# Expert rows added to their tokens in DRAM by an accumulating scatter, in a perceiver layer with a mixture of experts

## The chip, the core and the metric

The kernel runs on one core of one Trainium2 chip. The time is device microseconds of one execution, first to last instruction plus what lies around them. Times before: 2608.23, 2605.57 and 2600.91 us, median 2605.57 us. The profile is of a separate execution of 2611.01 us.

The core has a matrix engine (PE), a vector engine (DVE), an activation engine (ACT), a general engine (POOL, also called GpSimd) and a queue engine (SP) that only issues transfers. Each takes its instructions in a fixed order, and an instruction that waits holds up all behind it. Transfers (DMA) run on 16 engines of their own, whoever issues them.

## The reference, cut to what matters

One layer of a perceiver with 512 tokens of width 512: cross attention on a context of 8192 rows, a state-space block with its MLP, and a mixture of experts.

```python
x = x + xattn(layernorm(x), ctx, ctx, ...)      # 16 heads of 64, keys and values from ctx
x = x + ssm_and_mlp(layernorm(x), ...)          # scan over 512 tokens, then a gated MLP
x = x + ffn(layernorm(x), ...)

def ffn(x):                                     # 512 tokens, 16 experts, two per token
    top_vals, top_idx = top_k(x @ router_w.T, 2)
    gates = sigmoid(top_vals)
    # moe[n] = sum over the two experts e of token n: gate * (silu(x gate_e) * (x up_e)) @ down_e
    return moe + (silu(x @ sg.T) * (x @ su.T)) @ sd.T       # plus one shared expert
```

Every weight and the data are float32. The kernel splits each operand into a high and a low float16 half and takes three matmuls for a product (high by high, high by low, low by high).

## The kernel before

**First pass of the attention (`filler`).** Heads are taken in pairs, two pairs a pass. In the first pass the 8192 context rows come in 16 chunks of 512. `ctx_first` loads a chunk in float32 (L230), splits it (L232 to L235) and writes the halves to DRAM for later passes (L236). `kproj_units` and `vproj_units` project keys and values (L251 to L253, L275 to L277) and write them to DRAM. `smax_units` takes a first score with the high halves only (L300), copied by ACT (L305), for a running maximum on DVE (L311, L313). After chunk 0 `first_norm` normalises x and `qproj` projects the queries; the scores of chunk 0 are then spread between the projections of chunk 1. The order on PE is written out by hand in this part: a generator yields its parts, and a list `side` holds score work from which `pump` takes a piece every few projections. On the other engines a scheduler orders the instructions. Weights are loaded by `stage_w` and split by `split_w` (L176, L177).

**Main pass.** Scores, exponentials and products with V, unit by unit, with the projections of later passes filled in by a rate. Beside it `weight_prep` zeroes DRAM scratch and splits the later weights. This takes the time from about 240 to 2100 us. The tail, with the state-space block, the MLP, the router and the experts, follows.

**Router and experts.** The expert of a token is found from the logits; a running count gives each (token, choice) a slot in a table of 23 blocks of 128 rows (16 experts and 7 blocks for overflow). `sg` holds these slots, `gt` the gates. Eight indirect transfers on POOL (L1201), one per group of 128 tokens and choice, scatter the split rows (`xf`, 2 KB each) into the DRAM table `xd_d`. They all write one tensor, so each waits for the one before. `moe_in` loads the 128 rows of a block through SP (L1208), transposes them on PE (L1212) and copies them (`xk`). `moe_up` and `moe_down` do the matmuls (L1225, L1250), `moe_turn` the transposes between; the result is scaled on ACT (`myo`, L1256) and written by SP to row block k of `y_d` (L1257). Weights come in pieces of 512 KB through SP (`wef`, L1089) and are split by ACT and DVE (L1094, L1095) into `we` (18 buffers) or `wpm` (5 buffers, which the shared expert's weights use too, L761). The shared expert (`ffn`, L966 to L978) runs while the scatters go.

Eighteen blocks always run; five more stand behind a test of the overflow count.

**The end.** Eight indirect gathers on POOL (L1285) fetch each token's two results from `y_d`; DVE multiplies by the gate and adds to `x_sb` (L1289); SP writes four output blocks (L1292).

Of the kernel before, what the change touches and what calls it, by code (L numbers as in the profile page):

```python
# [9 lines left out]
F32 = mybir.dt.float32  # L10
AF = mybir.ActivationFunctionType
# [5 lines left out]
P = 128  # L17
# [17 lines left out]
LAST = 8000  # L35


@with_exitstack
def perceiver_layer(ctx: ExitStack, tc: tile.TileContext, a: dict, out: bass.AP):
# [23 lines left out]
    y_d = scr.tile([(16 + NOV) * P, DM], F32, name="y_d")  # L63
    xd_d = scr.tile([(16 + NOV) * P, 2 * DM], F16, name="xd_d")
# [98 lines left out]
    nc.sync.dma_start(bq_sb, a["bq"])  # L163
    nc.sync.dma_start(bk_sb, a["bk"])
    nc.sync.dma_start(bv_sb, a["bv"])
    nc.vector.tensor_scalar(bk_sb, bk_sb, WS, None, ALU.mult)

    def stage_w(src, n, tag, stage=("wst", 1), bufs=2):
        st = sb2.tile([P, NC4, n], F32, name=f"wst_{tag}", tag=stage[0], bufs=stage[1])
        nc.sync.dma_start(st, src)  # L170
        return lambda: split_w(st, n, tag, bufs)
# [254 lines left out]
    def filler():  # L426
# [23 lines left out]
        for g in range(NPASS):  # L450
            pr = (2 * g, 2 * g + 1)
            if g == 0:
                wk0 = load_w(a["Wk"][0], P, "k", bufs=4)
                nct = ctx_first(0)
                wk = [wk0, load_w(a["Wk"][1], P, "k", ("p32", 3), bufs=4)]
                wv = load_w(a["Wv"][0], 256, "v", ("p32", 3))
                nc.sync.dma_start(x_sb, a["x"])
                wq = [load_w(a["Wq"][p], P, "q", ("t2k", 4)) for p in pr]
            else:
                wk, wv, wq = nw  # L460
                qh = [qproj(p, w) for p, w in zip(pr, wq)]
                yield 2 * 2592
            runm = [None, None]
            ks = [[None] * NCH for _ in pr]
            for c in range(NCH):
# [6 lines left out]
                if nxt < NPASS * NCH:  # L472
                    nct = ctx_first(nxt) if nxt < NCH else ctx_load(nxt % NCH)
# [9 lines left out]
                if g == 0 and c == 0:  # L483
                    first_norm()
                    qh = [qproj(p, w) for p, w in zip(pr, wq)]
                    yield 2 * 2592
                if c == 2:
                    for p, q in zip(pr, qh):
                        qplace(p, *q)
                side += [smax_units(c, i, qh[i][0], ks[i][c], runm, g == 0) for i in range(2)]  # L490
# [117 lines left out]
    for m in range(NSTEP):  # L608
        n = NLAST * NSTEP + m
        if m % 4 == 0:  # L610
            load(n // 4 + 1)
        cur = scores(u, m, loads[n // 4], sp, True)
        while len(pend) > 1:
            drain()
        pend.append((u, m, cur))
        if m == 0:
            tl = tail(tc, a, out, const, scr, ident, x_sb, mlp_d, oT, y_d, xd_d, (ps_s, ps_o, ps_x, bank_j))
        for _ in range(2):
            if m >= 1 and not ready:
                ready = next(tl)  # L620
# [12 lines left out]
def tail(tc, a, out, const, scr, ident, x_sb, mlp_d, oT, y_d, xd_d, psums):  # L633
# [494 lines left out]
    xf = const.tile([P, 4, 2, DM], F16, name="xf", tag="big16")  # L1128
    nc.scalar.copy(xf[:, :, 0, :], u_sb)
    nc.vector.tensor_tensor(xf[:, :, 1, :], u_sb, xf[:, :, 0, :], ALU.subtract)  # L1130
# [68 lines left out]
    for i in range(4):  # L1199
        for j in range(2):  # L1200
            nc.gpsimd.indirect_dma_start(  # L1201
                out=xd_d[:], out_offset=bass.IndirectOffsetOnAxis(ap=sg[:, j, i : i + 1], axis=0),
                in_=xf[:, i].rearrange("p x d -> p (x d)"), in_offset=None,
            )

    def moe_in(k):
        xd = g2.tile([P, 2, NC4, P], F16, name="xd", bufs=3)
        nc.sync.dma_start(xd, xd_d[k * P : (k + 1) * P, :].rearrange("t (x d m) -> t x d m", x=2, d=NC4))  # L1208
        pt = bank_j([P, 2, NC4, P], F16, "pxd")
        for x in range(2):  # L1210
            for d in range(NC4):
                nc.tensor.transpose(pt[:, x, d, :], xd[:, x, d, :], id16)  # L1212
        xk = g2.tile([P, 2, NC4, P], F16, name="xk", bufs=2)
        nc.scalar.copy(xk, pt)
        return xk
# [30 lines left out]
    def moe_down(k, gT, ws):  # L1246
# [9 lines left out]
        nc.scalar.activation(yo, py, AF.Copy, scale=IW)  # L1256
        nc.sync.dma_start(y_d[k * P : (k + 1) * P, :], yo)  # L1257
# [24 lines left out]
    for i in range(4):  # L1282
        for j in range(2):
            yg = g2.tile([P, DM], F32, name="yg", tag="yo", bufs=4)
            nc.gpsimd.indirect_dma_start(  # L1285
                out=yg, out_offset=None, in_=y_d[:],
                in_offset=bass.IndirectOffsetOnAxis(ap=sg[:, j, i : i + 1], axis=0),
            )
            nc.vector.scalar_tensor_tensor(  # L1289
                x_sb[:, i, :], yg, gt[:, i, j : j + 1], x_sb[:, i, :], ALU.mult, ALU.add  # L1290
            )
        nc.sync.dma_start(out[:, i, :], x_sb[:, i, :])  # L1292
# [69 lines left out]
```

## Time and profile before

| what | value |
|---|---|
| median of three runs | 2605.57 us (2600.91 to 2608.23) |
| the profiled execution | 2611.01 us, its span 2609.3 us |
| busy share of PE, DVE, ACT, POOL | 91%, 79%, 75%, 2% |
| granted PE clock, mean | 0.973 |
| DMA, moved and mean rate | 531.43 MB, 204 GB/s |
| transfers of SP's queue | 352148 packets, 523.69 MB |
| transfers of POOL's queue | 1280 packets, 4.20 MB |

The page of a profile shows the span in 40 slices, the busy groups of instructions, and the chain of work that ended last. A timeline row gives start, length, engine, line, operation, output and input, and in brackets how long the engine stood idle before it and what ended that. A row of the waits gives the waiting instruction, what released it, and the sum, the number and the longest in us. SPq is SP issuing a transfer; POOL's DMA_INDIRECT is the making of a transfer's descriptors, and the transfer itself follows. PE's matmuls overlap: rows of 0.38 us start every 0.216 us.

### The profile page before, as it was taken

Reading aid. Unit: us, or ns where it says so; the run is one execution under the profiler, and the core shown is the slowest. Engines: PE = TensorE matmul, PEld = TensorE weight load, DVE = VectorE, ACT = ScalarE, POOL = GpSimd, SP = SyncE. Lnnn points to the kernel's source line nnn. Section 1 sums busy time; section 2 is a strip of 40 time slices with the busy share of each in tenths; the row PEclk is TensorE's granted clock in tenths of the full one; section 3 lists DMA queues with packets and bytes.
Section 4 is the critical chain, followed back from the end, with each engine's and each line's share of the span. In section 5 each row is a group of like instructions: output and inputs, shape, how many; then the busy total and the mean of one; then the engine's idle time right before and its main releaser. Section 6 shows DMA issues by size and latency. Waiting matters only on the chain. (4 is left out here: it accounts for less than half of the span.)

```text
span 2609.3 us, 54424 instructions
## 1 busy us (share of the span) xinstructions
PE 2383.2 (91%) x21806; PEld 1676.5 (64%) x21806; DVE 2062.4 (79%) x2403; ACT 1949.2 (75%) x3734; POOL 44.3 (2%) x58
## 2 busy tenths in 40 slices
PE   7999899999999999999999998997877688998895
PEld 3555577776677777767777777995665466665442
DVE  6776588888888888878888778997899999533785
ACT  5787788888788888868888888997776476333784
POOL 2000000000000000000000000000000000001001
PEclk9999999999999999999999999999989899999998
DMA  7974677778687778778877655877510222766896
GB/s 270 312 259 138 231 212 231 229 235 241 199 234 235 226 221 251 226 199 228 236 221 213 175 156 148 207 205 192 159 41 25 97 81 82 260 225 217 293 331 208
DMA packets 353688, 531.43 MB, mean 204 GB/s; under 512 B 25107, under 2 KB 218835, under 8 KB 353301
## 3 DMA queue, kind: packets, MB, share of 16 engines
q1 hardware_dynamic: 352148, 523.69, 65.8%
q0 software_dynamic: 1280, 4.20, 0.5%
q8 instruction: 173, 2.83, 0.5%
q14 instruction: 87, 0.70, 0.1%
HBM read 397.68 MB, written 126.94 MB: 201 GB/s over the span
## 5 line engine op out<-in xcount | busy, mean ns | idle before, releaser
L377 DVE TENSOR_TENSOR phl<-p,phl 128x1024 f16<-128x1024 f32 x512 | 626.7, 1225 | 193.2 <-ACT phl L374 181.0
L372 ACT ACTIVATE p<-pss 128x512 f32<-128x512 f32 x1024 | 597.7, 622 | 114.5 <-PE pss L365 42.2
L305 ACT ACTIVATE sf<-psx 128x512 f16<-128x512 f32 x1024 | 558.5, 625 | 70.9 <-PE psx L300 70.1
L364 PE MATMUL pss<-qhh,k 128*128 128x256 f16 x2048 | 481.0, 275 | 14.3 <-ACT phl L374 12.0
L365 PE MATMUL pss<-qlm,kb 128*128 128x256 f16 x2048 | 479.7, 274 | 0.9 <-DMA kb<-k_d 0.9
L313 DVE TENSOR_TENSOR runm<-runm,sf 128x2048 f16<-128x2048 f16 x240 | 292.3, 1219 | 51.7 <-ACT sf L305 51.5
L394 PE MATMUL po<-v,phl 128*128 128x130 f16 x4096 | 322.7, 220 | 3.9 <-DVE oq L407 3.4
L374 ACT ACTIVATE phl<-pss 128x512 f16<-128x512 f32 x512 | 312.8, 611 | 0.0
L394 PEld LDWEIGHTS <-phl 128*128 128x128 f16 x4096 | 271.0, 98 | 61.6 <-issue 14.8
L275 PE MATMUL psv<-wh_v,ctxc 128*128 128x256 f16 x1024 | 282.0, 275 | 7.3 <-ACT wh_v L176 3.2
L276 PE MATMUL psv<-wl_v,ctxc 128*128 128x256 f16 x1024 | 280.8, 274 | 1.2 <-DVE wl_v L177 1.2
L277 PE MATMUL psv<-wh_v,ctxc 128*128 128x256 f16 x1024 | 280.9, 274 | 0.0
L364 PEld LDWEIGHTS <-k 128*128 128x128 f16 x2048 | 200.9, 98 | 66.0 <-issue 20.0
L365 PEld LDWEIGHTS <-kb 128*128 128x128 f16 x2048 | 201.4, 98 | 53.0 <-issue 14.6
L300 PE MATMUL psx<-khl,qh 64*128 64x512 f16 x1024 | 208.9, 386 | 17.6 <-ACT sf L305 12.2
L922 PE MATMUL py<-hs,ident 128*128 128x256 f32 x512 | 144.0, 437 | 73.5 <-DVE hs L919 73.5
L397 PE MATMUL po<-v,phl 128*128 128x65 f16 x4096 | 208.5, 193 | 2.5 <-DVE phl L377 2.5
L251 PE MATMUL psk<-ctxc,wh_k 128*128 128x512 f16 x512 | 198.0, 387 | 9.9 <-ACT ctxc L234 8.1
L376 DVE CAST phl<-p 128x1024 f16<-128x1024 f32 x256 | 176.0, 687 | 32.2 <-ACT p L372 32.0
L252 PE MATMUL psk<-ctxc,wh_k 128*128 128x512 f16 x512 | 196.3, 383 | 0.8 <-DVE ctxc L235 0.7
L253 PE MATMUL psk<-ctxc,wl_k 128*128 128x512 f16 x512 | 196.3, 383 | 0.0
L922 PEld LDWEIGHTS py<-hs,ident 128*128 128x128 f32 x512 | 107.2, 217 | 107.0 <-DVE hs L919 87.0
(304 smaller groups left out, 3774.6 us busy)
## 6 DMA issues: line engine op xcount, KB each, us to landing
v<-v_d SPq DMA_DIRECT2D x128, 520.0 KB
k<-k_d SPq DMA_DIRECT2D x256, 256.0 KB
ctxc<-ctx_d SPq DMA_DIRECT2D x96, 512.0 KB
wef<-in_gu_dram SPq DMA_DIRECT2D x72, 512.0 KB
v_d<-vs SPq DMA_DIRECT2D x128, 260.0 KB
k_d<-khl SPq DMA_DIRECT2D x128, 256.0 KB
kb<-k_d SPq DMA_DIRECT2D x128, 256.0 KB
wpm<-w_d SPq DMA_DIRECT2D x48, 512.0 KB
```

The lines of the kernel that those rows point to most:

```text
L275: nc.tensor.matmul(ps[:, t, :], lhsT=ct[i // 2][:, 0, i % 2, sl], rhs=wh[:, i, :], start=i == 0, stop=False)
L276: nc.tensor.matmul(ps[:, t, :], lhsT=ct[i // 2][:, 0, i % 2, sl], rhs=wl[:, i, :], start=False, stop=False)
L277: nc.tensor.matmul(ps[:, t, :], lhsT=ct[i // 2][:, 1, i % 2, sl], rhs=wh[:, i, :], start=False, stop=i == NC4 - 1)
L305: nc.scalar.activation(dst, ps, AF.Copy, scale=1.0 / (8.0 * WS))
L313: nc.vector.tensor_tensor(r, r, sf, ALU.max)
L364: nc.tensor.matmul(ps[:, hh], lhsT=k[:, hh, sl], rhs=qhh[:, hh, qs], start=True, stop=False)
L365: nc.tensor.matmul(ps[:, hh], lhsT=b[:, hh, sl], rhs=qlm[:, hh, qs], start=False, stop=True)
L372: nc.scalar.activation(p32[:, i], pss[i], AF.Exp, scale=sc)
L374: nc.scalar.activation(ph[:, i], pss[i], AF.Exp, scale=sc)
L377: nc.vector.tensor_tensor(pl, p32, ph, ALU.subtract)
L394: nc.tensor.matmul(o, lhsT=ph[:, i, hh, qs], rhs=vv, start=first, stop=False, **kw)
L922: nc.tensor.matmul(py[:, j, :], lhsT=ident, rhs=hs[:, n, 1:], start=k == 0, stop=False)
```

## The change

Three parts, of which the first is in no summary of it.

1. **First pass.** The loads of the biases `bq`, `bk`, `bv` move from the head of SP's queue to where they are needed. The second K weights and the V weights are loaded right after chunk 0, into buffers that the main pass uses later, then chunk 1, then x and the Q weights. The first norm and the Q projection move from after chunk 0 to after chunk 1, and the scores of chunk 0 come straight after them, drained before chunk 2.
2. **Scatters.** A row of `xd_d` grows by 8 bytes to `XR` = 1028 halfwords: the token's row number and its gate over 64 (`IW`). Empty slots get, in `weight_prep`, the number of one of 128 spare rows and a zero gate. The eight scatters are declared independent of each other, and go by choice: the gate column of `xf` is written for choice 0, four scatters, then for choice 1, four scatters. Every load of `xd` waits for all eight.
3. **Experts and end.** Rows are loaded, and results stored, through POOL's queue. The store is an indirect transfer that adds the 128 rows, scaled by their gates, to the rows of `sum_d`; `sum_d` is set to `x_sb` before the first. The gathers and adds at the end are gone: `sum_d` is copied to the output from DRAM to DRAM.

In the built program POOL's order among the experts is: the eight scatters, the row loads of experts 0 to 3, then in turn the add of expert k and the row load of expert k+4. That load waits for the add (it reuses its buffer); each add waits for the one before.

```diff
+XR = 2 * DM + 4
-    y_d = scr.tile([(16 + NOV) * P, DM], F32, name="y_d")
-    xd_d = scr.tile([(16 + NOV) * P, 2 * DM], F16, name="xd_d")
+    sum_d = scr.tile([NQ + P, DM], F32, name="sum_d")
+    xd_d = scr.tile([(16 + NOV) * P, XR], U16, name="xd_d")
...
-    nc.sync.dma_start(bq_sb, a["bq"])
-    nc.sync.dma_start(bk_sb, a["bk"])
-    nc.sync.dma_start(bv_sb, a["bv"])
-    nc.vector.tensor_scalar(bk_sb, bk_sb, WS, None, ALU.mult)
...
-                wk = [wk0, load_w(a["Wk"][1], P, "k", ("p32", 3), bufs=4)]
-                wv = load_w(a["Wv"][0], 256, "v", ("p32", 3))
+                wk1, wv = stage_w(a["Wk"][1], P, "k", ("k", 2), bufs=4), stage_w(a["Wv"][0], 256, "v", ("k", 2))
+                nc.sync.dma_start(bk_sb, a["bk"])
+                nc.vector.tensor_scalar(bk_sb, bk_sb, WS, None, ALU.mult)
+                nxt0 = ctx_first(1)
+                wk, wv = [wk0, wk1()], wv()
                 nc.sync.dma_start(x_sb, a["x"])
-                wq = [load_w(a["Wq"][p], P, "q", ("t2k", 4)) for p in pr]
+                wq = [stage_w(a["Wq"][p], P, "q", ("v", 3)) for p in pr]
+                nc.sync.dma_start(bq_sb, a["bq"])
+                nc.sync.dma_start(bv_sb, a["bv"])
...
-                if g == 0 and c == 0:
+                if g == 0 and c == 1:
                     first_norm()
-                    qh = [qproj(p, w) for p, w in zip(pr, wq)]
+                    qh = [qproj(p, w()) for p, w in zip(pr, wq)]
                     yield 2 * 2592
+                    side += [smax_units(0, i, qh[i][0], ks[i][0], runm, True) for i in range(2)]
...
-                side += [smax_units(c, i, qh[i][0], ks[i][c], runm, g == 0) for i in range(2)]
+                if g or c:
+                    side += [smax_units(c, i, qh[i][0], ks[i][c], runm, g == 0) for i in range(2)]
+                if (g, c) == (0, 1):
+                    while len(side) > 2:
+                        yield from pump()
...
+        none = sb2.tile([P, 2, 1], mybir.dt.int32, name="none", bufs=1)
+        nc.gpsimd.memset(none, 0)
+        nc.gpsimd.iota(none[:, 0], pattern=[[0, 1]], base=NQ, channel_multiplier=1)
         for k in range(16 + NOV):
-            nc.sync.dma_start(xd_d[k * P : (k + 1) * P, :], zero)
-            if k >= 16 + MOV:
-                nc.sync.dma_start(y_d[k * P : (k + 1) * P, :], zero.bitcast(F32))
+            rows = slice(k * P, (k + 1) * P)
+            nc.sync.dma_start(xd_d[rows, 0 : 2 * DM], zero.bitcast(U16))
+            nc.sync.dma_start(xd_d[rows, 2 * DM : XR], none.rearrange("p a o -> p (a o)").bitcast(U16))
...
+        nc.sync.dma_start(sum_d[NQ : NQ + P, :], zero.bitcast(F32))
...
+    sent = []
+    for j in range(2):
+        nc.vector.tensor_scalar(xf[:, :, XR - 2 : XR].bitcast(F32), gt[:, :, j : j + 1], IW, None, ALU.mult)
+        for i in range(4):
+            d = nc.gpsimd.indirect_dma_start(
                 out=xd_d[:], out_offset=bass.IndirectOffsetOnAxis(ap=sg[:, j, i : i + 1], axis=0),
-                in_=xf[:, i].rearrange("p x d -> p (x d)"), in_offset=None,
+                in_=xf[:, i], in_offset=None,
             )
+            for o in sent:
+                tc.declare_no_dep(d.ins, o.ins, reason="every slot is one token's: the rows differ")
+            sent.append(d)
...
-        xd = g2.tile([P, 2, NC4, P], F16, name="xd", bufs=3)
-        nc.sync.dma_start(xd, xd_d[k * P : (k + 1) * P, :].rearrange("t (x d m) -> t x d m", x=2, d=NC4))
+        xd = g2.tile([P, XR], U16, name="xd", bufs=4)
+        r = nc.gpsimd.dma_start(xd, xd_d[k * P : (k + 1) * P, :])
...
-        nc.scalar.activation(yo, py, AF.Copy, scale=IW)
-        nc.sync.dma_start(y_d[k * P : (k + 1) * P, :], yo)
+        row, gate_ = slot.pop(k)
+        nc.scalar.activation(yo, py, AF.Copy, scale=gate_)
+        nc.gpsimd.indirect_dma_start(
+            out=sum_d[:], out_offset=bass.IndirectOffsetOnAxis(ap=row, axis=0), in_=yo, in_offset=None,
+            compute_op=ALU.add,
+        )
...
+    nc.sync.dma_start(sum_d[0:NQ].rearrange("(p i) d -> p i d", i=4), x_sb)
     moe(range(16 + MOV), lambda k: expert(k) if k < 16 else overflow(regs[k - 16]))
...
-    for i in range(4):
-        for j in range(2):
-            yg = g2.tile([P, DM], F32, name="yg", tag="yo", bufs=4)
-            nc.gpsimd.indirect_dma_start(
-                out=yg, out_offset=None, in_=y_d[:],
-                in_offset=bass.IndirectOffsetOnAxis(ap=sg[:, j, i : i + 1], axis=0),
-            )
-            nc.vector.scalar_tensor_tensor(
-                x_sb[:, i, :], yg, gt[:, i, j : j + 1], x_sb[:, i, :], ALU.mult, ALU.add
-            )
-        nc.sync.dma_start(out[:, i, :], x_sb[:, i, :])
+    nc.sync.dma_start(out, sum_d[0:NQ].rearrange("(p i) d -> p i d", i=4))
```

More of the change, by code (lines that the diff above doesn't have):

```diff
@@ L10 @@
 F32 = mybir.dt.float32
+U16 = mybir.dt.uint16
 AF = mybir.ActivationFunctionType
@@ L162, in perceiver_layer @@
     bv_sb = L.tile([P, NPAIR], F32, name="bv_sb")
-    nc.sync.dma_start(bq_sb, a["bq"])
-    nc.sync.dma_start(bk_sb, a["bk"])
-    nc.sync.dma_start(bv_sb, a["bv"])
-    nc.vector.tensor_scalar(bk_sb, bk_sb, WS, None, ALU.mult)
     def stage_w(src, n, tag, stage=("wst", 1), bufs=2):
-        st = sb2.tile([P, NC4, n], F32, name=f"wst_{tag}", tag=stage[0], bufs=stage[1])
+        pool = L if stage[0] in ("k", "v") else sb2
+        st = pool.tile([P, NC4, n], F32, name=f"wst_{tag}", tag=stage[0], bufs=stage[1])
         nc.sync.dma_start(st, src)
@@ L471, in filler @@
                 nxt = g * NCH + c + 1
-                if nxt < NPASS * NCH:
+                if nxt == 1:
+                    nct = nxt0
+                elif nxt < NPASS * NCH:
                     nct = ctx_first(nxt) if nxt < NCH else ctx_load(nxt % NCH)
@@ L616, in perceiver_layer @@
         if m == 0:
-            tl = tail(tc, a, out, const, scr, ident, x_sb, mlp_d, oT, y_d, xd_d, (ps_s, ps_o, ps_x, bank_j))
+            tl = tail(tc, a, out, const, scr, ident, x_sb, mlp_d, oT, sum_d, xd_d, (ps_s, ps_o, ps_x, bank_j))
         for _ in range(2):
@@ L630, in perceiver_layer, with tail @@
         pass
-def tail(tc, a, out, const, scr, ident, x_sb, mlp_d, oT, y_d, xd_d, psums):
+def tail(tc, a, out, const, scr, ident, x_sb, mlp_d, oT, sum_d, xd_d, psums):
     nc = tc.nc
@@ L1127, in tail @@
     ln2(1, xT1, lambda: next(rs0, None))
-    xf = const.tile([P, 4, 2, DM], F16, name="xf", tag="big16")
-    nc.scalar.copy(xf[:, :, 0, :], u_sb)
-    nc.vector.tensor_tensor(xf[:, :, 1, :], u_sb, xf[:, :, 0, :], ALU.subtract)
+    xf = const.tile([P, 4, XR], U16, name="xf", tag="big16")
+    xv = xf[:, :, 0 : 2 * DM].bitcast(F16)
+    nc.scalar.copy(xv[:, :, 0:DM], u_sb)
+    nc.vector.tensor_tensor(xv[:, :, DM : 2 * DM], u_sb, xv[:, :, 0:DM], ALU.subtract)
+    nc.gpsimd.iota(xf[:, :, 2 * DM : 2 * DM + 2].bitcast(I32), pattern=[[1, 4], [0, 1]], base=0, channel_multiplier=4)
     mx = G.tile([P, 4, 8], F32, name="mx8")
@@ L1197, in tail @@
     nc.vector.tensor_copy(oii, oid)
-    for i in range(4):
-        for j in range(2):
-            nc.gpsimd.indirect_dma_start(
+    sent = []
[3 more added lines that the diff above has]
+            d = nc.gpsimd.indirect_dma_start(
                 out=xd_d[:], out_offset=bass.IndirectOffsetOnAxis(ap=sg[:, j, i : i + 1], axis=0),
-                in_=xf[:, i].rearrange("p x d -> p (x d)"), in_offset=None,
+                in_=xf[:, i], in_offset=None,
             )
+            for o in sent:
+                tc.declare_no_dep(d.ins, o.ins, reason="every slot is one token's: the rows differ")
+            sent.append(d)
+    slot = {}
     def moe_in(k):
-        xd = g2.tile([P, 2, NC4, P], F16, name="xd", bufs=3)
-        nc.sync.dma_start(xd, xd_d[k * P : (k + 1) * P, :].rearrange("t (x d m) -> t x d m", x=2, d=NC4))
+        xd = g2.tile([P, XR], U16, name="xd", bufs=4)
+        r = nc.gpsimd.dma_start(xd, xd_d[k * P : (k + 1) * P, :])
+        for o in sent:
+            tc.add_manual_dep(
+                r.ins, o.ins.name, mybir.DependencyInfo(mybir.DependencyClass.Sync, mybir.DependencyReason.DATA),
+                reason="rows of every scatter",
+            )
         pt = bank_j([P, 2, NC4, P], F16, "pxd")
@@ L1211, in moe_in @@
             for d in range(NC4):
-                nc.tensor.transpose(pt[:, x, d, :], xd[:, x, d, :], id16)
+                o = x * DM + d * P
+                nc.tensor.transpose(pt[:, x, d, :], xd[:, o : o + P].bitcast(F16), id16)
         xk = g2.tile([P, 2, NC4, P], F16, name="xk", bufs=2)
         nc.scalar.copy(xk, pt)
+        slot[k] = xd[:, 2 * DM : 2 * DM + 2].bitcast(U32), xd[:, 2 * DM + 2 : XR].bitcast(F32)
         return xk
@@ L1255, in moe_down @@
         yo = g2.tile([P, DM], F32, name="myo", tag="yo", bufs=4)
-        nc.scalar.activation(yo, py, AF.Copy, scale=IW)
-        nc.sync.dma_start(y_d[k * P : (k + 1) * P, :], yo)
+        row, gate_ = slot.pop(k)
[3 more added lines that the diff above has]
+            compute_op=ALU.add,
+        )
     def moe(ks, weights):
@@ L1281, in tail @@
         moe(range(16 + MOV, 16 + NOV), lambda k: overflow(regs[k - 16]))
-    for i in range(4):
-        for j in range(2):
-            yg = g2.tile([P, DM], F32, name="yg", tag="yo", bufs=4)
-            nc.gpsimd.indirect_dma_start(
-                out=yg, out_offset=None, in_=y_d[:],
-                in_offset=bass.IndirectOffsetOnAxis(ap=sg[:, j, i : i + 1], axis=0),
-            )
-            nc.vector.scalar_tensor_tensor(
-                x_sb[:, i, :], yg, gt[:, i, j : j + 1], x_sb[:, i, :], ALU.mult, ALU.add
-            )
-        nc.sync.dma_start(out[:, i, :], x_sb[:, i, :])
+    nc.sync.dma_start(out, sum_d[0:NQ].rearrange("(p i) d -> p i d", i=4))
     es.close()
```

## The prediction

> **What bounds the kernel now.** I read the 40 slices first: PE is 9 tenths busy nearly everywhere, so time can be won only where PE waits and nothing else makes up for it. The change touches three such places: the first 50 us, the router with the scatters of the token rows, and the experts with the end. For each I asked the timeline and the waits who is late. 0.3% of 2605.57 us, 7.8 us, is about what a measurement can tell from no change.
>
> *The start.* Idle time of PE by releaser, window 0 to 20 us, then 20 to 40 (waited for: us, times, longest):
>
> ```profile
> PE psk L251 <- ACT ctxc L234: 8.1, 1, 8.1
> PE psv L275 <- ACT wh_v L176: 3.2, 1, 3.2
> PE psv L276 <- DVE wl_v L177: 1.2, 1, 1.2
> ```
>
> PE starts at 8.12 us, and stops again at 17 us for the V weights.
>
> *The scatters.* Timelines of POOL and SP, and PE's waits from 2352 to 2400 us:
>
> ```profile
> 2352.83 1.15 POOL L1201 DMA_INDIRECT xd_d<-xf,sg  x1 [135.70 <-DVE sg L1184]
> 2356.02 0.97 POOL L1201 DMA_INDIRECT xd_d<-xf,sg  x1 [2.04 <-DMA xd_d<-xf,sg]
> 2362.56 0.96 POOL L1201 DMA_INDIRECT xd_d<-xf,sg  x1 [5.57 <-DMA xd_d<-xf,sg]
> ...
> 2384.12 0.95 POOL L1201 DMA_INDIRECT xd_d<-xf,sg  x1 [2.01 <-DMA xd_d<-xf,sg]
> 2387.22 1.31 SPq L1208 DMA_DIRECT2D xd<-xd_d  x3
> 2388.64 0.37 SPq L761 DMA_DIRECT2D wpm<-rsu_d  x1
> PE pu L703 <- DMA wpm<-rsu_d: 8.8, 1, 8.8
> ```
>
> Each scatter waits for the one before, so eight take 34 us. SP stands at the first load of rows (L1208) until 2387.2; the last weights of the shared expert (rsu_d) are queued behind it, and PE waits 8.8 us for them.
>
> *The experts.* Waits of SP and ACT from 2400 to 2586 us, and one window (length; busy us of PE, PEld, DVE, ACT, POOL; PE clock, DMA share, GB/s):
>
> ```profile
> SPq L1257 <- ACT myo L1256: 66.8, 17, 9.2
> ACT we L1094 <- DMA wef<-in_gu_dram: 20.8, 19, 3.0
> 2500.00:2547.00 47.00, 45.53 (x267) 22.07 (x266) 40.74 (x43) 38.80 (x49) 0.00 (x0) 1.00 0.91 333
> ```
>
> Here PE, DVE, ACT and DMA are all within 18% of full. The copies of the result (myo, L1256) start at 2421.19 and 2585.97 us for the first and the eighteenth: 164.8 us for 17 steps, 9.7 each, but 8.7 to 9.0 where nothing waits. In SP's queue, weight loads stand behind the write of each result (66.8 us in all, much of it harmless because the weight buffers are full).
>
> *The end.* Timeline:
>
> ```profile
> 2585.97 0.60 ACT L1256 ACTIVATE myo<-acc 128x512 f32<-128x512 f32 x1 [6.03 <-PE acc L1250]
> 2591.14 0.98 POOL L1285 DMA_INDIRECT yg<-y_d,sg  x1 [206.07 <-SPq L1280]
> ...
> 2600.84 0.95 POOL L1285 DMA_INDIRECT yg<-y_d,sg  x1 [0.30 <-issue]
> 2604.52 1.54 DVE L1289 SCALAR_TENSOR_TENSOR x_sb<-yg,gt,x_sb 128x512 f32<-128x512 f32 x2 [1.44 <-DMA yg<-y_d,sg]
> ```
>
> From the last result to the end of the span: 2609.3 - 2586.6 = 22.7 us, in which PE does nothing.
>
> **Part 1, the start (moved): -3.5 us.** The three bias loads leave the head of SP's queue (issues at 0.81, 1.27 and 1.73 us; the first weight follows at 2.21), so everything starts 1.4 us earlier. The V weights are issued right behind the second K weights instead of behind x and two ctx_d writes; at the rate of the first loads (cf and the second K weights arrived by 10.7 us) they are in at about 11 us, and PE's waits of 3.2 and 1.2 us go. PE then also avoids running V at half clock after the stall (spacing 0.215 instead of 0.108 us for 12 matmuls, 1.3 us). Sum of gains 7.1. Against it: the norm and the Q projection now come after chunk 1, and chunk 0's scores (16 matmuls, 16 copies L305) follow in one block that no projection covers. Before, chunk 1 held those scores and took 13.0 us on PE (37.2 to 50.2). Now it takes 10.4 without them (24 matmuls of 0.216, 48 of 0.109 us), and the block 6.2: the copies need 16 x 0.51 = 8.2 us on ACT (four take 2.05), and four PSUM banks let PE leave some 2 us before their end. Loss 3.6. Net -3.5, between -5 and 0 (DMA is 0.96 busy from 60 to 85 us and could give some back). What follows until 2100 us is bound by PE and shifts along. 23 small writes of row numbers into xd_d and one zeroed block of sum_d replace five zeroed blocks of y_d; they lie in that stretch, where DMA is 0.67 busy (300 to 2100 us): nothing. If SP were late there, 23 x 0.33 us of issue would count, 8 us.
>
> **Part 2, unordered scatters: -4 us.** Without waits POOL issues at the spacing of the gathers (2591.14 to 2600.84, 7 steps: 1.39 us). But the gate of the second choice is written into the same xf, so that write on DVE waits until the first four scatters have landed. Issued from 2352.8 to 2357.0, with 2.7 to 6.3 us to landing (3.8 median, from the scatters' rows), they are done at about 2362. Behind it on DVE is the split of gg (L970, due at 2357.1), and PE's matmuls L711 wait for that: a new stall of 4.8 us (3 to 7). The other four scatters then land by 2372, the row loads on POOL by 2376, before PE wants rows at 2395. The 8.8 us stall goes, as SP has no row loads any more and rsu_d is issued when its buffer frees. -8.8 + 4.8 = -4.0.
>
> **Part 3, experts' rows and results on POOL's queue: -4 us.** One rule speaks against a gain. The row: SP waits 66.8 us for myo with weights queued behind, and ACT waits 20.8 us for weights. The Trainium skill, *DMA: Bandwidth & Descriptors*, "Rules for kernel authors", says that spreading DMAs over SP, ACT and GpSimd for bandwidth does not help, as all run on the same 16 engines. By it the gain is 0, and the extra bytes cost. By the row, the slow steps (2421.19 to 2464.08 us: 42.9 for four) could come to 9.2 each, -6, and the last three (29.1 us, DMA late) lose up to 1.5 more. Issue, not bandwidth, is what is freed: DMA was 0.86 to 0.88 busy in those slow steps. I take the row, but charge the bytes of part 4.
>
> **Part 4, the add in DRAM (not in the trace).** 18 adds of 256 KB read the destination too: 18 x 0.26 = 4.7 MB, at 333 GB/s 14 us of DMA time if DMA bound every step; it has 9 to 14% free over 165 us (15 to 23 us), so I charge half of the 7.6 us of part 3, which leaves 4. The second question is the round trip. In POOL's order each add is followed by the row load four experts on, which waits for that add (it reuses its buffer), and then by the next add. A step therefore lasts at least the add's landing plus 1.3 us. Nearest row: the plain scatter (L1201) of the same 256 KB, 2.7 us quiet, 6.3 us under load. The skill's *Collectives: The Full Stack*, "The bandwidth ceiling: the fold count and why AG ≠ RS ≠ AR", says an add is 2 reads for 1 write and halves the rate. By the row alone 6.3 us; by the rule the moving part doubles (about 1.6 us more, estimated from 256 KB in five packets per engine at the trace's 0.163 us a packet, each taking turns with one of SP's), so 8 us. Bounds 4 and 12. I take 7: a step of 8.3, below PE's 9. Cost 0.
>
> **Part 5, the end: -9.7 us.** Gone: the write's landing, eight gathers, eight adds on DVE, four output writes (22.7 us). New: the last add starts 0.3 us after the result, lands 4.5 us later in a quiet memory (2.7 to 9), SP issues the copy (0.5), and 1 MB goes from DRAM to DRAM. No row has that; 1 MB at the best slice of the trace (383 GB/s) takes 2.7 us, twice that if read and write share the engines, and a write needs about 3 us to land (2606.4 to 2609.3): 5 to 9, I take 7.7 because a DMA of sixteen 64 KB rows is new here. Sum 13.0, gain 9.7 (3 to 14).
>
> **Sum.** -3.5 - 4 - 4 - 9.7 = -21 us on the profiled execution (2611.01 us, span 2609.3), giving 2590. The median of the runs is 5.4 us below that execution: 2605.6 - 21 = **2584 us**.
>
> **Rivals.**
>
> *A, as forecast* (0.58): 2572 to 2596.
>
> *B, the experts give nothing and the scatters' new wait eats the old stall* (0.22). For it: DVE stands in order behind four scatters, and DMA is 0.91 busy where the experts go well. Against it: two of three stalls are queue order, not bytes. Start and end remain, 13 us; less 2 for a slower stage: 2594.
>
> *C, the add's round trip becomes the bound* (0.20, the other side). Place: POOL's queue between add and row load. Each step costs landing + 1.3 us. It decides against the change when 17 steps exceed 164.8 us plus the 12 us won elsewhere (3.5 + 4 + about 4.7 at an end slowed by the same landing): a landing above 9.1 us. At 10 us: 17 x 11.3 = 192, +27 - 12 = +15, so 2620; at 12 us 2650. For it: an add reads first, DMA is full, and no row shows it. Against it: no plain scatter took over 6.3 us. The spare results and rows (four buffers each) only delay it.
>
> **Chances and range.** Faster by over 0.3% (below 2597.8 us): nearly all of A and three quarters of B, 0.73. Within 0.3%: the rest of B and the edge of C, 0.08. Slower: 0.19. Range 2572 to 2613: A's lower end (experts -8, end -13) up to C's first half.
>
> **What would show it.** Start right: V's first matmul near 15.5 us with no wait, chunk 2's K projection near 46.5 instead of 50.2. Scatters: a DVE wait of about 5 us at the second gate write, no PE wait for rsu_d, first expert's transposes 4 us earlier plus the start's shift. Experts: results every 9.2 to 9.5 us. Add: landing under 8 us, POOL idle before row loads but PE never waiting for xd. End: about 13 us from the last result. Wrong if PE waits on xd in every expert (C), or if DMA stays above 0.95 and ACT's wait for weights grows (B).

## The result and the profile after

| | before | after |
|---|---|---|
| median | 2605.84 us (20 runs) | 2610.32 us (20 runs) |
| ratio | 1 | 1.0018, 95% interval 1.0010 to 1.0027 |
| profiled execution, its span | 2611.01, 2609.3 us | 2607.09, 2605.4 us |
| POOL's queue | 1280 packets, 4.20 MB | 4672 packets, 11.56 MB |

The change costs 4.7 us (2.6 to 7.0), where 21 us of gain were forecast. Single executions of one kernel lie some 6 us to either side of the median, and the two profiled ones lie the other way round (3.9 us). So spans are not compared below; each stage is measured from a mark at its head, and the verdicts come from the ratios. 0.001 of the ratio is 2.6 us.

**Start.** V's first matmul comes at 15.92 us without a wait, where 15.5 was forecast. The next trouble lies behind chunk 1, where x is now normalised and transposed. PE's timeline in the kernel before (first transposes, chunk 1), and in the changed one (transposes, scores, chunk 2):

```profile
28.30 0.60 PE L100 MATMUL pt_x<-ident,xn 128*128 128x128 f32 x4
...
37.22 0.38 PE L251 MATMUL psk<-ctxc,wh_k 128*128 128x512 f16 x1
```

```profile
31.66 1.61 PE L102 MATMUL pt_x<-ident,xn 128*128 128x128 f32 x4
...
37.32 1.12 PE L102 MATMUL pt_x<-ident,xn 128*128 128x128 f32 x4 [3.13 <-DVE vs L281]
...
46.53 0.61 PE L299 MATMUL psx<-khl,qh 64*128 64x512 f16 x4
47.86 7.92 PE L299 MATMUL psx<-khl,qh 64*128 64x512 f16 x16 [0.72 <-ACT sf L304]
55.72 0.61 PE L250 MATMUL psk<-ctxc,wh_k 128*128 128x512 f16 x1
```

PE stands 3.13 us because DVE, in order, is still at V's sums and the splits of the next chunk. Transposes and Q projection take 14.9 us (31.66 to 46.53), where they took 8.9 before (28.30 to 37.22). The block of scores then lasts 9.2 us (46.53 to 55.72; forecast 6.2). It holds 20 scores, not 16: when a piece is used up, `pump` goes on to the next, so the loop that drains chunk 0 also takes the first four scores of chunk 1. Chunk 2's K projection starts at 55.7 us: 50.2 before, 46.5 forecast. The windows of 20 to 60 us (length; busy us of PE, PEld, DVE, ACT, POOL; PE clock, DMA share, GB/s), first before, then after:

```profile
20.00:40.00 20.00, 17.34 (x102) 10.56 (x103) 17.56 (x23) 9.00 (x14) 7.19 (x5) 0.91 0.79 283
40.00:60.00 20.00, 18.60 (x111) 8.83 (x110) 11.85 (x15) 15.61 (x31) 0.00 (x0) 1.00 0.77 259
```

```profile
20.00:40.00 20.00, 15.67 (x102) 10.57 (x100) 16.18 (x30) 8.08 (x13) 1.64 (x2) 0.89 0.89 297
40.00:60.00 20.00, 18.93 (x56) 5.85 (x55) 10.55 (x15) 13.84 (x25) 4.25 (x4) 0.68 0.72 228
```

From 40 to 60 us PE is as busy as before but does 56 recorded matmuls in place of 111, at a granted clock of 0.68. A mark further on is ACT's first copy of K in the fifteenth chunk: 227.2 us before, 231.1 after.

**Scatters.** Waits of the changed kernel from 2350 to 2370 us (waited for: us, times, longest), and POOL's timeline:

```profile
DVE xf L1218 <- DMA xd_d<-xf,sg: 8.1, 1, 8.1
...
PE acc L726 <- DVE gg L985: 7.4, 1, 7.4
```

```profile
2354.89 0.96 POOL L1220 DMA_INDIRECT xd_d<-xf,sg  x1 [0.30 <-issue]
2362.93 1.15 POOL L1220 DMA_INDIRECT xd_d<-xf,sg  x1 [7.09 <-DVE xf L1218]
...
2373.27 2.20 POOL L1233 DMA_DIRECT2D xd<-xd_d  x4 [5.40 <-DMA xd_d<-xf,sg]
```

The four scatters go out back to back and the old wait for rsu_d is gone. But the second gate column (L1218) waits for all four, the split of gg stands behind it on DVE, and PE waits 7.4 us, which had been put at 4.8. From SP's first load of the shared expert's gate weights (rsg_d), which heads the stage, to the first expert's transposes it is 86.8 us in place of 88.9: a gain of 2.1 us in this execution.

**Experts.** From the first expert's transposes to the start of the last result: 2395.4 to 2590.5 us, 195.1 in place of 186.4. From first to eighteenth result: 171.4 in place of 164.8. Four waits of the changed kernel from 2395 to 2606 us, and the adds (issue in ns, min/median/max; then the time to landing):

```profile
POOL xd L1233 <- DMA sum_d<-myo,xd: 68.5, 11, 7.4
ACT we L1109 <- DMA wef<-in_gu_dram: 34.1, 34, 3.7
...
PE pxd L1243 <- ACT mg L1262: 12.8, 7, 3.2
...
PE pxd L1243 <- DMA xd<-xd_d: 2.2, 2, 1.5
```

```profile
L1290 POOL DMA_INDIRECT sum_d<-myo,xd x18: 1544/1822/2220, 2420.1 to 2593.0; - x18
...
DMA to landing us min/median/max: 4.7/7.9/9.1
```

The add lands in 7.9 us at the median, near the 7 that was taken, and PE waits only 2.2 us in all for rows (xd). What PE waits for is ACT, and ACT stands 34 times at pieces of weights that have not landed; before it was 20.8 us, 19 times. To see where in the stage the loss lies, the windows of the first three steps and of the rest (same columns), before and after:

```profile
2421.20:2450.20 29.00, 25.94 (x156) 12.98 (x154) 22.07 (x23) 21.31 (x28) 0.00 (x0) 1.00 0.87 298
2450.20:2586.00 135.80, 121.28 (x687) 58.12 (x685) 106.41 (x110) 99.22 (x122) 0.00 (x0) 0.97 0.82 296
```

```profile
2419.20:2454.50 35.30, 30.54 (x171) 14.56 (x170) 23.88 (x25) 22.42 (x29) 7.41 (x6) 0.90 0.90 263
2454.50:2590.60 136.10, 119.16 (x666) 57.65 (x663) 105.65 (x108) 99.96 (x121) 30.95 (x25) 0.96 0.89 294
```

Three steps take 35.3 us in place of 29.0, with the DMA engines busier (0.90), at 263 GB/s (a figure that leaves out what the adds read, as the last section shows), and with a PE clock of 0.90. ACT's wait for pieces in these steps, before and after:

```profile
ACT we L1094 <- DMA wef<-in_gu_dram: 4.8, 3, 2.4
```

```profile
ACT we L1109 <- DMA wef<-in_gu_dram: 8.8, 4, 2.7
```

The fourteen steps that follow take what they took in these two executions. The experts of the kernel before also run, unchanged in their code, in `e_start`, `e_loads` and `e_loads2`, and there the fourteen last 131.0 to 132.4 us. So a single execution tells this stretch only to some 5 us.

**End.** Timeline of the changed kernel:

```profile
2587.48 1.54 POOL L1290 DMA_INDIRECT sum_d<-myo,xd  x1 [6.57 <-ACT myo L1289]
...
2590.52 0.69 ACT L1289 ACTIVATE myo<-acc,xd 128x512 f32<-128x512 f32 x1 [3.31 <-PE acc L1282]
2593.00 1.55 POOL L1290 DMA_INDIRECT sum_d<-myo,xd  x1 [3.97 <-issue]
2599.06 0.61 SPq L1319 DMA_DIRECT2D out_dram<-sum_d  x1
```

14.2 us from the last result to the end of the span (2591.2 to 2605.4), in place of 22.7. The last add starts 1.8 us after the result, because the one before it must land first: where the adds go in turn to two tables (`e_two_xd7`, below), it starts 0.3 us after.

```profile
2578.28 0.69 ACT L1290 ACTIVATE myo<-acc,xd 128x512 f32<-128x512 f32 x1 [3.31 <-PE acc L1283]
...
2579.25 1.55 POOL L1291 DMA_INDIRECT sum_d<-myo,xd  x1 [2.45 <-ACT myo L1290]
```

### The profile page after: what moved, and what is told of

It is laid out like the page before. It is cut to its first block, busy times and chain, and to the rows that moved or that the text cites. A ratio compares the mean times of both kernels' runs of the same rounds, so it can differ in the third digit from the quotient of the medians.

```text
span 2605.4 us, 54442 instructions
## 1 busy us (share of the span) xinstructions
PE 2386.2 (92%) x21806; PEld 1678.3 (64%) x21806; DVE 2055.6 (79%) x2397; ACT 1950.5 (75%) x3734; POOL 77.1 (3%) x89
## 3 DMA queue, kind: packets, MB, share of 16 engines
q0 software_dynamic: 4672, 11.56, 2.0%
## 5 line engine op out<-in xcount | busy, mean ns | idle before, releaser
L393 PEld LDWEIGHTS <-phl 128*128 128x128 f16 x4096 | 271.7, 98 | 61.9 <-issue 14.8
L364 PEld LDWEIGHTS <-kb 128*128 128x128 f16 x2048 | 201.2, 98 | 52.0 <-issue 14.2
L375 DVE CAST phl<-p 128x1024 f16<-128x1024 f32 x256 | 175.9, 687 | 31.8 <-ACT p L371 31.6
L396 PEld LDWEIGHTS <-phl 128*128 128x128 f16 x4096 | 171.2, 97 | 4.3 <-DVE phl L376 3.6
```

What stands on the lines that cost most here:

```text
L364: nc.tensor.matmul(ps[:, hh], lhsT=b[:, hh, sl], rhs=qlm[:, hh, qs], start=False, stop=True)
L393: nc.tensor.matmul(o, lhsT=ph[:, i, hh, qs], rhs=vv, start=first, stop=False, **kw)
L396: nc.tensor.matmul(o, lhsT=pl[:, i, hh, qs], rhs=vv_, start=False, stop=last, **kw)
```

## The experiments

Each ratio is to the kernel before, from five rounds on one chip, with its 95% interval. Not all kernels ran on the same chip, so kernels are compared by their ratios, and a difference of two ratios carries both intervals.

### The start alone, and the change without it

The pieces are those of part 1 of the change, put into the kernel before (`e_start`) or taken out of the changed one (`e_oldstart`):

```diff
-                if g == 0 and c == 0:
+                if g == 0 and c == 1:
                     first_norm()
```

> The kernel before with the change's first part alone (bias loads, V weights early, first norm and Q projection after chunk 1, chunk 0's scores in one block). Theory L (the late norm and Q projection stall PE and lower its clock): chunk 2's K projection near 55.8 us as in the changed kernel, against 50.2, and the whole +4 us, ratio 1.0015. Forecast: 46.5 us and -3.5 us, ratio 0.9987.

> The changed kernel with the first part undone. Theory L: 4 us faster than the changed kernel, so level with the kernel before (ratio 1.000). Forecast: 3.5 us slower than the changed kernel, ratio 1.003.

Measured: 1.0008 (1.0000 to 1.0015) and 1.0010 (1.0002 to 1.0018). Both put the start at about +2 us, and the forecast's -3.5 is excluded by the first. The mark at the fifteenth chunk is steadier than the totals: in the twelve runs with the new start it lies at 230.5 to 233.5 us, mean 232.0, and in the five with the old one at 227.2 to 229.8, mean 228.7. So the start costs 3.2 us there. In the profiled execution the changed kernel had caught up by the fifth chunk (90.1 against 90.2 us), and lost the time again up to the seventh, where DMA was 0.98 busy from 90 to 125 us (0.91 before). Why just there was not tried.

### Only the early weights

`e_loads` moves the loads and leaves norm and Q projection after chunk 0. `e_loads2` also puts x and the Q weights ahead of chunk 1 (in outline; where the weights are split is left out):

```diff
-                nxt0 = ctx_first(1)
                 nc.sync.dma_start(x_sb, a["x"])
                 wq = [stage_w(a["Wq"][p], P, "q", ("v", 3)) for p in pr]
+                nxt0 = ctx_first(1)
```

> The kernel before with the early half of the first part alone: bias loads late, second K weights and V weights right behind chunk 0, chunk 1 before x and the Q weights; the first norm and the Q projection stay after chunk 0. If the late norm alone makes the start lose: PE's waits for the V weights go (4.4 us), chunk 2's K projection near 46 us, the whole 3 to 5 us less than before, ratio 0.998 to 0.999. Rival (the Q weights and x, now behind chunk 1, come late for the norm after chunk 0): PE waits in the Q projection instead, chunk 2 at 50 us or later, ratio 1.000 or more.

> As e_loads, with x and the Q weights issued ahead of chunk 1. If e_loads gained nothing because x came behind chunk 1 (PE stood 5.8 us for the normalised x), that wait goes too: chunk 2's K projection at 45 to 47 us, the whole 3 to 5 us less than before, ratio 0.998 to 0.999. Rival: chunk 1 is late in turn, or DVE is, and the ratio stays at 1.000.

Measured: 1.0003 (0.9995 to 1.0011) and 1.0035 (1.0022 to 1.0049). The first gains nothing and the second, meant to mend it, is the worst start of all, with the mark at 234.0 us. PE waits for DVE's xn 5.8 us in one and 5.7 in the other:

```profile
PE pt_x L100 <- DVE xn L81: 5.7, 1, 5.7
PE psx L297 <- ACT sf L302: 1.7, 1, 1.7
```

(the waits of PE in `e_loads2` from 20 to 60 us). The 4.4 us that PE stood for the V weights in the kernel before had been cover: while it stood, DVE normalised x (statistics from 13.2 us, xn from 19.6). The wait went, and one for DVE took its place. That the order of the loads was the whole cause is thereby refuted.

### The gate column on POOL

```diff
-        nc.vector.tensor_scalar(xf[:, :, XR - 2 : XR].bitcast(F32), ...
+        nc.gpsimd.tensor_scalar(xf[:, :, XR - 2 : XR].bitcast(F32), ...
```

> The changed kernel with the two gate columns written on POOL in place of DVE, so that only POOL, which waits there anyway, stands behind the first four scatters. Theory G (DVE's wait is what eats the gain of the scatters): PE's wait of 7.4 us for gg goes, the first expert's transposes come 5 to 7 us earlier after the first scatter (38 to 40 us in place of 44.5), and the whole is 5 to 7 us less than the changed kernel, ratio to before 0.9995. Rival: the experts' weights come no sooner, and what is won here is waited for among the experts: under 2 us less, ratio 1.001 or more.

Measured: 0.9990 (0.9981 to 0.9998), 7.3 us (4 to 10 by the two intervals) less than the changed kernel. Waits of PE from 2340 to 2405 us in it:

```profile
PE acc L724 <- ACT gg L984: 1.4, 1, 1.4
PE pg L718 <- DMA wpm<-rsg_d: 0.9, 1, 0.9
PE acc L726 <- DVE gg L985: 0.3, 1, 0.3
```

The 7.4 us are gone, and the stage is 79.9 us long in place of 86.8. One instruction of 0.17 us, on the wrong engine, had cost all that the unordered scatters won.

### Unordered scatters alone

`e_scat_rows` is the kernel before with two edits only (and the scatters in order of choice):

```diff
+            for o in sent:
+                tc.declare_no_dep(d.ins, o.ins, reason="every slot is one token's: the rows differ")
-        nc.sync.dma_start(xd, xd_d[k * P : (k + 1) * P, :]...
+        r = nc.gpsimd.dma_start(xd, xd_d[k * P : (k + 1) * P, :]...
```

> The kernel before with unordered scatters and row loads on POOL alone; rows of 2 KB without number and gate, so no gate column is written; results still stored by SP to a table of their own and gathered at the end. Theory G: the 8.8 us wait for rsu_d goes and no wait on DVE takes its place: 6 to 9 us less than before, ratio 0.9965 to 0.998. Rival: the experts take it back because weights arrive no sooner, ratio 0.999 or more.

Measured: 0.9968 (0.9957 to 0.9980), 8.3 us less than before. It is the fastest of the kernels here that leave nothing out, and it beats the kernel before and the changed one. `e_best` adds the start of `e_loads2` to it:

> e_scat_rows with the start of e_loads2: if both gains hold and add up, 11 to 13 us less than before, ratio 0.995 to 0.996; if the start gives nothing, 0.997 as e_scat_rows.

1.0002 (0.9991 to 1.0012): the same start costs the same 9 us in another kernel.

### Plain stores, and bytes in place of the add

`e_plain` drops `compute_op=ALU.add`. `e_read` and `e_read2` add to it 18 loads of 256 KB that nothing reads:

```diff
+        more = g2.tile([P, DM], F32, name="more", bufs=2)
+        r = nc.gpsimd.dma_start(more, a["gu"][:, k % 16, 0:DM])
+        tc.add_manual_dep(r.ins, res.ins.name, ...)        # e_read2 only: after the expert's result
```

> The changed kernel with plain stores in place of adding ones (leaves out the sum: a token's row holds its last result only). Theories B (the add's reads of the old rows fill the DMA engines, which are the bound) and R (each add waits for the one before, 8 us landing and 2 us of issue, and so sets the step of 10 us): the experts' results come every 9.2 us or less in place of 10.1, the end is 2 us shorter, the whole 10 to 17 us less than the changed kernel, ratio to before 0.995 to 0.998. Rival Q (the queues' new order costs it, rows on POOL and weights running ahead on SP): the experts stay at 10 us a step and only the end's 2 us are won, ratio 1.001.

> The changed kernel with plain stores (leaves out the sum, as e_plain) plus a load of 256 KB per expert through POOL's queue into buffers that nothing reads. Theory B (what the add costs is the DMA time of its reads): the 5 us that plain stores gave are lost again, ratio 1.001 to 1.003. Theory R (the add's own round trip): as e_plain, ratio 0.999 to 1.0005.

> As e_read, with each extra load of 256 KB made to wait for the result of its expert: in e_read they had all run before the experts, so that run was e_plain once more. Theory B (what the add costs is the DMA time of its reads): ratio 1.0015 to 1.003, the results 171 us from first to eighteenth. Theory R (the add's own round trip): as e_plain, 0.9995 to 1.0008.

Measured: `e_plain` 0.9998 (0.9988 to 1.0008), 5.2 us (1.8 to 8.6 by the two intervals) less than the changed kernel. In `e_read` the loads ran at 2227 to 2291 us, before the experts, so it is `e_plain` a second time: 1.0005 (0.9995 to 1.0015). `e_read2` holds them in the experts: 1.0022 (1.0011 to 1.0032), 4.4 us (0.5 to 8.3) more than `e_read` for the same loads at another time. First three steps and the rest, `e_plain` and then `e_read2`:

```profile
2424.10:2457.10 33.00, 29.16 (x160) 14.29 (x159) 23.77 (x25) 22.49 (x28) 5.47 (x6) 0.90 0.84 279
2457.10:2589.50 132.40, 117.60 (x678) 57.16 (x675) 106.08 (x108) 99.45 (x121) 22.92 (x25) 0.99 0.84 304
```

```profile
2422.60:2458.60 36.00, 30.68 (x175) 15.17 (x174) 23.90 (x25) 22.46 (x29) 7.14 (x9) 0.95 0.86 288
2458.60:2594.30 135.70, 115.80 (x661) 55.78 (x659) 106.08 (x108) 99.75 (x121) 30.74 (x39) 0.99 0.86 319
```

256 KB more to read per expert, with no add, lengthen both windows, and cost about what the adds cost. PE waits for no row in `e_read2`, so it is not late rows. That speaks for theory B: the price of 18 adds is some 5 us, and their reads alone can account for it. And `e_plain` itself answers the other half: with no add, and SP freed of results and rows, results still take 165.4 us from first to eighteenth (163.7 in `e_read`), against 159.8 to 164.8 in the four kernels with the experts of before. The freed queue alone brings nothing.

The stages of all kernels that share these parts, each from single executions (the scatters from the first load of rsg_d to the first transposes, the experts from there to the start of the last result, the end behind that result):

| kernels | scatters | experts | first three steps | end |
|---|---|---|---|---|
| as before (`before`, `e_start`, `e_loads`, `e_loads2`) | 88.3 to 89.1 us | 181.7 to 186.4 | 28.1 to 29.0 | 22.0 to 22.9 |
| unordered scatters, rows on POOL (`e_scat_rows`, `e_best`) | 79.0 to 79.3 | 187.1 to 189.2 | 31.6 to 32.0 | 22.2 to 22.4 |
| all of parts 2 and 3, plain stores (`e_plain`, `e_read`) | 86.3 to 88.6 | 187.0 to 188.3 | 32.2 to 33.0 | 12.9 to 13.5 |
| the same with adds (`after`, `e_oldstart`) | 86.8 to 89.6 | 193.2 to 195.1 | 35.3 to 36.1 | 14.2 to 14.8 |

So the adds bring about half of what the first three steps lose. The other half is there without any add, once scatters are unordered and rows come through POOL's queue, which is what rival Q of `e_plain` had in mind. Which of the two makes it, and how, was not tried.

### Is it the round trip of the adds?

`e_two` lets experts add in turn into two tables, and copies row number and gate out of the rows. `e_two_xd7` has seven row buffers in place of the copies (in both, the output leaves out the second table), `e_xd7` the seven buffers with one table, and `e_two_sum` two tables that are added at the end, with the old start:

```diff
-            out=sum_d[:], out_offset=bass.IndirectOffsetOnAxis(ap=row, axis=0), in_=yo, in_offset=None,
+            out=sum_d[k % 2][:], out_offset=bass.IndirectOffsetOnAxis(ap=row, axis=0), in_=yo, in_offset=None,
-                    w = g2.tile([P, 2, 1024], F16, name="we", bufs=18)
+                    w = g2.tile([P, 2, 1024], F16, name="we", bufs=16)
-        xd = g2.tile([P, XR], U16, name="xd", bufs=4)
+        xd = g2.tile([P, XR], U16, name="xd", bufs=7)
```

> The gates on POOL, and the round trip broken: the experts add in turn into two tables (the output leaves out the second table), so that an add waits only for the one two before it, and row number and gate are copied out of the rows, so that a row load waits for no add. The bytes are the same. Theory R (round trip): results every 9.2 us or less, 157 us from first to eighteenth, ratio to before 0.994. Theories B and H: 168 to 172 us as with the gates on POOL alone, ratio 0.998 to 1.000.

> As e_two, with seven buffers for the rows in place of the copies on DVE, which in e_two stood waiting for rows 29 us in all; two of the 18 buffers of split pieces pay for it, which by e_stage costs nothing. An add waits only for the one two before it, a row load for an add seven before. Theory R: results 157 to 163 us from first to eighteenth, ratio to before 0.994 to 0.997. Theory B: 168 to 173 us, ratio 0.9985 to 1.0005.

> The changed kernel with the gates on POOL, one table, and seven row buffers in place of four (16 buffers of split pieces in place of 18). A row load now waits for an add seven experts back, but each add still waits for the one before. If the row load's wait in POOL's queue is the link that costs: results 158 to 164 us from first to eighteenth, ratio 0.995 to 0.9975, as e_two_xd7. If the chain from add to add is the link: 168 to 173 us, ratio 0.998 to 1.000, as with the gates on POOL alone.

> e_two_xd7 made whole: the second table starts from zero, and at the end the two are loaded, added on DVE and written out; the first part of the change is undone. From e_two_xd7 (0.9959) the old start takes 2 us off and the longer end adds 2 to 5 us: ratio 0.995 to 0.997, the end 16 to 19 us after the last result. If the gain of e_two_xd7 was not the chain, 0.999.

| | ratio | first three steps | the rest |
|---|---|---|---|
| e_gatepool (base of these) | 0.9990 | 36.3 us | 134.8 us |
| e_two | 1.0048 (1.0035 to 1.0061) | 31.1 | 140.8 |
| e_two_xd7 | 0.9959 (0.9945 to 0.9974) | 28.2 | 133.5 |
| e_xd7 | 0.9987 (0.9976 to 0.9998) | 35.4 | 131.3 |
| e_two_sum | 0.9995 (0.9982 to 1.0007) | 35.2 | 134.1 |

`e_two` missed by far: its copies stand on DVE for rows that have not landed, 29.3 us in all, and PE waits 13.8 us for DVE's mgT, which stands behind them. `e_two_xd7` met what the round trip foretold, 8 us less. But `e_two_sum` breaks the same two links and its experts take 169.3 us from first to last, near the 171.1 of the base (its end lasts 19.6 us, which uses up what the old start wins). `e_xd7` breaks one link and its ratio moves by less than its interval. So the round trip is not what `e_two_xd7` won: in the profiled executions 8.1 of its 9.5 us lie in the first three steps. There its order on ACT differs. In the built programs the scheduler has put one split of weights between the first two experts' activations (mg) in `e_two_xd7`, three in `e_two_sum`. ACT's wait for pieces in these steps of `e_two_xd7`, and their window:

```profile
ACT we L1110 <- DMA wef<-in_gu_dram: 1.6, 4, 0.9
```

```profile
2416.60:2444.80 28.20, 25.43 (x154) 12.72 (x152) 24.44 (x26) 23.48 (x30) 6.80 (x5) 1.00 0.97 313
```

1.6 us, against 8.8 in the changed kernel and 4.8 in the kernel before; three steps in 28.2 us against 35.3 and 29.0. The same adds are there. `e_two` has the order of `e_two_xd7`, and its three steps are short too (31.1). That ACT's order makes the difference between these kernels is read from their traces; an order written by hand was not tried. The order is not what sets the changed kernel apart from the kernel before: that one has three splits in this place as well, and takes 29.0 us. With the same order, the pieces are waited for longer.

### Pacing the weights, and deeper staging

The lead of the loads over the experts (pieces issued when a result starts, less six for each result so far) falls from 25 to 9 in the kernel before, as SP stands at results, and stays at 18 to 25 in the changed one up to its last three steps. `e_pace` forces a falling lead, `e_stage` gives two more staging buffers:

```diff
+                if 31 <= nload[0] < 108:
+                    tc.add_manual_dep(r.ins, results[int((nload[0] - 31) / 5.2)].ins.name, ...)
```

> The changed kernel with the gate columns on POOL, and each load of a weight piece from the 32nd on (of 108) made to wait for the result of an earlier expert, 5.2 pieces to an expert, so that the lead of the loads is used up evenly, as in the kernel before. Theory H (ACT works in order: in the changed kernel it splits six pieces a step, 16 pieces ahead of PE, and stands at pieces that are not needed for two more experts, with the copies PE needs behind it): results come every 9.0 to 9.4 us, 153 to 162 us from the first to the eighteenth in place of 171, the whole 9 to 15 us less than with the gates on POOL alone, ratio to before 0.993 to 0.9955. Theories B (bytes) and R (the adds' round trip): nothing changes, ratio 0.999.

> As e_pace, with the first part of the change undone as well. If the late norm costs what the runs with and without it showed, 2 to 3 us less than e_pace. Theory H then gives a ratio of 0.992 to 0.995, theories B and R 0.998.

> As e_pace, with plain stores in place of adding ones (leaves out the sum: a token's row holds its last result only). Theory H with little left for the bytes: 2 to 4 us less than e_pace, ratio 0.992 to 0.994. Theory B: at least 10 us less than e_pace, ratio 0.995 where e_pace has 0.999.

> The changed kernel with the gates on POOL, and eight staging buffers for weight pieces in place of six, paid for with two of the 18 buffers of split pieces. Theory H (ACT stands in order at pieces that have not landed, because a piece is only issued when the sixth before it has been split): ACT's waits for wef fall from 35 us to 20 or less, the results come 0.3 to 0.5 us earlier per expert, 5 to 9 us in all, ratio 0.9955 to 0.997. Theory B (the bytes are the bound): 0.999 as without it.

Measured: 1.0003 (0.9992 to 1.0014), 0.9987 (0.9978 to 0.9996), 0.9961 (0.9948 to 0.9974) and 0.9998 (0.9990 to 1.0007). Pacing won nothing with adds. It takes hold only after the first three steps (lead 25, 24, 22, 22 as without it), which last 35.7 us still, and then only in part: at the fifteenth result the lead is 14, against 18 without it and 10 in the kernel before. Nor did two more staging buffers help: ACT's waits fell from 35 to 26 us and the three steps took 37.8. So theory H, that keeping too many pieces ahead costs time in every step, found no support, and it cannot explain the first three steps: there the lead is 25, 24, 22, 21 in the kernel before as well. A lead as low as that kernel's in the later steps was not tried. With plain stores the paced kernel is 11 us faster than with adds, twice the 5 us found without pacing. The intervals leave room for 6 to 15, so the two need not differ; if they do, why is open.

## Why the prediction was wrong, step by step

- **Part 1, -3.5 forecast, +3.2 at the mark (about +2 in the totals).** The first matmul came 0.9 us earlier (1.4 was counted) and the waits for V went. The step that failed is that norm and Q projection were moved at no cost: they took 14.9 us in place of 8.9. "PE's waits of 3.2 and 1.2 us go" asked what PE waited for, not what DVE did meanwhile, which was to normalise x. In the new place DVE is late with V's sums, and the projection begins at half clock. The second term is the block: 9.2 us in place of 6.2, as 16 scores were counted and 20 run.
- **Part 2, -4.0 forecast, -2.1 measured (-0.6 by the means given below).** The mechanism was right to the instruction. The term that was mis-sized is the wait at the second gate write: 4.8 us (3 to 7) taken, 7.4 on PE (8.7 in `e_oldstart`). The four scatters were thought to be down 9.2 us after the first issue and were down after 11.6.
- **Parts 3 and 4, -4 forecast, +8.7 measured (+11.1 by the means): the step that decided.** "I take the row" was wrong: SP's 66.8 us behind results were no loss, and their removal gave nothing (`e_plain`, 165.4 us against 164.8, the longest of the four with the experts of before). I called much of that wait harmless, and then priced the slow steps as if all of it had hurt. The rule that I weighed against it, that another queue brings no bandwidth, held. The bytes of the adds, charged 3.6 us, cost about 5 (4.4 by `e_read2`, 5.2 by `e_plain`). The rest shows in the first three steps, where ACT stands at weights; why it does so in kernels without adds stays open.
- **Part 4's round trip.** 7 us taken, 7.9 measured, and it was not the bound; rival C's place was wrong. POOL did wait on it (68.5 us), but the spare row buffers kept that from PE, which waited 2.2 us for rows. The estimate of 8 us with the moving part doubled was nearest.
- **Part 5, -9.7 forecast, -8.5 measured.** 14.2 us in place of 13.0, in part by luck. The last add starts 1.8 us after the result (0.3 taken), as it must wait for the one before. From its start to the issue of the copy it takes 6.1 us (4.5 taken). The copy itself was done 5.7 us after its issue (7.7 taken), which hid most of both.

Rival B came closest in kind (experts give nothing, the scatters' wait eats the stall), yet it kept 13 us from start and end. In the two profiled executions the stages sum to +3.2 - 2.1 + 8.7 - 8.5 = +1.3 us, where the ratio says +2.6 to +7.0. The kernel before took longer in the experts in its execution than the three others with the same experts. With the means of the table's first and last row (scatters 88.7 and 88.2 us, experts 183.1 and 194.1, end 22.6 and 14.5) the sum is +3.2 - 0.6 + 11.1 - 8.0 = +5.7 us, inside the interval.

## What to carry to other kernels

A wait of a queue or an engine is worth something only if what it frees is late itself: SP's 66.8 us were worth nothing, and PE's 4.4 us at the start were cover for DVE. When transfers are made independent, look for the small instruction that rewrites their source: it waits for all of them, and everything behind it on its engine waits too. Put it on the engine that would wait anyway. An accumulating store pays with DMA reads where the stage is full of weight loads (some 5 us here), and that has to be set against the saved end (8.5 us).

One execution per kernel can mislead about a stage: the same experts took 181.7 to 186.4 us in four kernels. Where several kernels share a stage, compare it over all of them.

## What the hardware showed that I had not expected

- An adding scatter of 128 rows of 2 KB keeps POOL 1.54 to 2.22 us (a plain one 0.96 to 1.56 in the same place) and lands in 4.7/7.9/9.1 us (min, median, max) against 3.2/6.0/7.4. Only its longest came to the 9.1 us from which it would have decided.
- A block of scores that is paced by ACT's copies went with half of PE's clock. In windows of 4 us the changed kernel has 0.50 and 0.68 behind the wait for DVE (36 to 44 us), 1.00 up to 48, and then 0.68, 0.50 and 0.54 through the block and into chunk 2's projection (48 to 60 us); the kernel before has 1.00 from 40 to 60. `e_start` repeats it (0.83, 0.50, 0.50 from 48 to 60 us). `e_loads2` has no such block, and falls to 0.50 from 56 to 60 us behind one wait of 1.7 us for the same copies. The Trainium skill, *TensorE: Matmul & The Clock Gate*, "What's actually happening", puts the drop behind an idle window of some 3.4 us. In the block no such gap is on record: sixteen matmuls in 7.9 us, one every half microsecond, went with it. How sparse the work must be was not tried.
- The GB/s of these views leave out what an add reads. POOL's queue in the page of the changed kernel, and of `e_plain`:

```profile
q0 software_dynamic: 4672, 11.56, 2.0%
```

```profile
q0 software_dynamic: 3520, 11.56, 1.2%
```

The bytes are the same with adds and without, but the adds have 1152 packets more. From 2460 to 2540 us the DMA engines show 0.98 busy at 334 GB/s with adds, 0.97 at 352 with plain stores, and 0.87 at 318 in the kernel before. An estimate from these: 4.72 MB of reads over the 171.4 us of the experts are 28 GB/s more, so 362 at 0.98 busy, which is 369 GB/s for a full share; plain stores give 363 and the kernel before 366. By this estimate the engines were not slower with adds; they moved bytes that the view does not count.
